# Layer 0 self-attention of a fused decoder: an earlier first unit of transposed scores, and the norm's scaling issued one step later

## The chip, the core and the metric

The kernel is one launch on one core of a Trainium2 chip. Its five engines, TensorE (PE), VectorE (DVE), ScalarE (ACT), GpSimd (POOL) and SyncE (SP, which here only starts DMAs), each run a list of instructions of their own that is fixed when the kernel is built, and wait for each other through semaphores. The metric is the device time of one execution in microseconds (us). Three runs of the kernel before have a median of 3543.11 us (3541.12 to 3548.39).

## The reference, cut to what matters

The program is a decoder of two layers over x of shape (8, 512, 256): self-attention, cross-attention and a feed-forward part in each layer, each followed by a residual add and a layer norm. The change touches only the first self-attention and its norm:

```python
def _L0_attn_ref(x, W_q, W_k, W_v, W_o, W_down_kv, W_up_k, W_up_v):
    q = x @ W_q
    k = x @ W_k
    v = x @ W_v
    latent_kv = (k + v) @ W_down_kv
    k_rec = (latent_kv @ W_up_k).reshape(b, s, H, HD).transpose(0, 2, 1, 3)
    v_rec = (latent_kv @ W_up_v).reshape(b, s, H, HD).transpose(0, 2, 1, 3)
    qh = q.reshape(b, s, H, HD).transpose(0, 2, 1, 3)
    scores = jnp.einsum('bhqd,bhkd->bhqk', qh, k_rec) / math.sqrt(d)
    decay = jnp.exp(-LAMBDA_DECAY * jnp.abs(t[:, None] - t[None, :]))
    scores = scores * decay[None, None, :, :]
    attn = jax.nn.softmax(scores, axis=-1)
    out = jnp.einsum('bhqk,bhkd->bhqd', attn, v_rec)
    return out.transpose(0, 2, 1, 3).reshape(b, s, d) @ W_o
...
x = _layernorm(x + _L0_attn_ref(x, ...), axis=-1)
```

There are 16 heads of 16 channels; the latent has 64 channels.

## The kernel before, in words

The stage works on 32 **units**: 8 batches, and in each batch 4 groups of 4 heads (`units`, in the order b, g). A unit takes four **steps**, kt = 0 to 3, one for each block of 128 keys. Everything is float32.

What one unit needs:

- `l0_prepare(b)`, once per batch and in four pieces: two turns of x (`turn`, four PE transposes of 128x128 into one PSUM tile `tT`, then an ACT copy to `xT`), `latent` (PE product with `wlat`, ACT copy) and `values` (PE product into an `s` tile, ACT copy to `vaug`). `wlat` is (W_k + W_v)^T times W_down: one DVE add of `wkT` and `wvT` (L557), eight recorded PE matmuls (L561), one DVE copy (L568).
- `l0_project` (L406 to L409): q and k of four heads by PE, two ACT copies.
- `l0_maxima(i)` (L423 to L438), for each of four blocks of 128 queries: the scores in plain layout by PE (`s_sc`, in two pairs, one `s` tile each), on each of four heads one DVE instruction that multiplies by the decay and takes the row maximum (`scored`, `mx`), then one DVE subtract that writes the block on the diagonal (`diag`, L438).
- `l0_shift` (L449 to L459): the negated maxima (DVE `mneg`), four PE transposes into `tM`, a DVE add into q (L455), and four POOL products `kr`, `kf`, `qf`, `qr` that carry the decay into q and k.
- `l0_probs(kt)` (L472 to L481): the transposed scores of one key block by PE into two `s` tiles, with the diagonal block transposed in from `diag`, and one ACT exponential for each tile (`pt`).
- `l0_values(kt)` (L492): PE adds the block's products with v to `o_pv`; the last one is copied out by ACT (`oT`, L501). `l0_finish` turns and divides.

The `s` tiles are three PSUM buffers used in turn, so each new one waits until the tile three places earlier has been read. The `tT`, `tM` and `o_out` tiles share one buffer.

**Order.** Before the loop the kernel computes `wlat`, prepares batch 0, projects units 0 and 1, takes all four maxima of unit 0, shifts it, takes all four maxima of unit 1, and projects unit 2. The loop then runs step kt of unit n as: transposed scores and exponentials of unit n; values of the step before; maxima number kt of unit n + 2; then, at kt = 1, the shift of unit n + 1; at kt = 2, `l0_finish` of unit n - 1; at kt = 0 and 3, one piece from the list `later`, and at kt = 3 also the projection of unit n + 3. `later` holds the next batch's `l0_prepare` and the last batch's `l0_output` (two turns, two products). The second product adds the residual (DVE, L541) and calls `normed(..., on_act=True)`: DVE statistics (L213, L214), a DVE add of epsilon (L215), a POOL power (`rs`, L216), a DVE product (`ve`, L218) and four ACT instructions that write the normed x (L221). Beside all this POOL runs a long chain of products for the feed-forward weights (`butterfly_ops`, L299), two or three of them per step, in a fixed order.

The four engines' lists come from a planner that sorts the instructions by priorities when the kernel is built; `tc.manual_schedule(engines={PE})` makes PE follow the order of the program inside its block, and `tc.keep_in_program_order(...)` does so for one instruction.

## Time and profile before

| what | value |
|---|---|
| median of three runs | 3543.11 us (3541.12 to 3548.39) |
| the profiled execution, time and span | 3548.88 us, of it 3547.2 us span |
| PE busy | 3332.7 us (94% of the span) |
| DVE, ACT, POOL busy | 2082.5, 1510.1, 1115.3 us (59%, 43%, 31%) |
| granted PE clock, mean | 0.965 of full |
| before the loop, up to the first transposed scores | 0 to 60.80 us |
| 28 intervals between ends of the loop's projections (82.02 to 780.15 us) | 698.13 us: PE busy 653.67, DVE 486.83, ACT 311.15, POOL 530.46 |

A row of the page or of the timeline gives the start in us, the duration, the engine, the line of the kernel, the operation, what is written and read, and how many instructions were merged; a bracket holds the idle time of the engine just ahead and what ended it. PE rows count each float32 matmul as two records. In the windows, columns are the stretch, its length, busy time and instruction count of PE, PEld (weight loads), DVE, ACT and POOL, then the granted PE clock (1.00 is full), the DMA share and GB/s. PE's ends are modelled, so a busy PE can still be a slow PE: the clock column has to be read beside it.

### The profile page before, as it was taken

The page shows a single profiled execution, that of the slowest core. Times are in us where ns is not written, and L with a number is a line of the kernel's source. Part 1 is how long each engine was busy: PE and PEld are TensorE (multiplying, and loading weights), DVE is VectorE, ACT ScalarE, POOL GpSimd, SP SyncE. Part 2 cuts the span into 40 slices and gives each one's busy share as a digit, 9 for nine tenths or more (in the row PEclk, how much of TensorE's full clock was granted, in tenths as well). Part 3 has the DMA queues.
Part 4 walks back from the last instruction along what each step waited for, and adds up shares of the span by engine and source line. Part 5 has one row for each costly group of instructions (what it writes and reads, how often), then busy time and mean ns, then how long its engine had stood idle before and what let it go on. Part 6 is the DMA issues. An engine that isn't in the chain of part 4 may idle for free. (4 is left out here: it accounts for less than half of the span.)

```text
span 3547.2 us, 52530 instructions
## 1 busy us (share of the span) xinstructions
PE 3332.7 (94%) x19574; PEld 2092.0 (59%) x19574; DVE 2082.5 (59%) x5710; ACT 1510.1 (43%) x3139; POOL 1115.3 (31%) x1032
## 2 busy tenths in 40 slices
PE   8989999998999989999999999999999998999995
PEld 3333434345666656666666666555555555888884
DVE  5777766675666556777777775666666665211012
ACT  2444444443443335655556654444444433222222
POOL 3868677772221122222222220011111111222222
PEclk8999999999999999999999999999999999999997
DMA  4100011111000079422333330000000004666674
GB/s 132 31 19 25 22 37 37 36 36 47 5 2 1 1 195 259 77 37 38 38 40 43 40 52 4 4 19 19 22 16 14 17 13 143 206 185 187 183 230 139
DMA packets 166001, 234.96 MB, mean 66 GB/s; under 512 B 26569, under 2 KB 128649, under 8 KB 165746
## 3 DMA queue, kind: packets, MB, share of 16 engines
q1 hardware_dynamic: 139010, 175.83, 15.8%
q0 software_dynamic: 25584, 51.57, 10.2%
q10 hardware_dynamic: 1152, 4.19, 0.3%
q8 instruction: 156, 2.56, 0.3%
q14 instruction: 99, 0.81, 0.1%
HBM read 135.83 MB, written 61.11 MB: 56 GB/s over the span
## 5 line engine op out<-in xcount | busy, mean ns | idle before, releaser
L428 DVE CUSTOM_DVE_ANT_0 scored<-s_sc,decay 128x512 f32<-128x512 f32 x512 | 323.5, 687 | 223.9 <-PE s_sc L423 222.7
L281 ACT ACTIVATE p<-p,nm 128x128 f32<-128x128 f32 (+3 forms) x512 | 282.5, 553 | 301.7 <-DVE nm L270 300.4
L865 POOL DMA_DIRECT2D qk<-turned x256 | 208.2, 1232 | 593.4 <-issue 304.6
L481 ACT ACTIVATE pt<-s_st 128x1024 f32<-128x1024 f32 x256 | 261.1, 1023 | 268.2 <-PE s_st L477 237.9
L902 DVE TENSOR_SCALAR p<-p,rsum 128x576 f32<-128x576 f32 (+4 forms) x768 | 300.3, 433 | 10.0
L1111 ACT ACTIVATE p<-s_sc,nm 128x576 f32<-128x576 f32 x256 | 189.6, 743 | 221.7 <-DVE nm L1110 200.8
L1477 DVE TENSOR_SCALAR y<-o_y,share 128x256 f32<-128x256 f32 x71 | 34.2, 483 | 408.9 <-PE o_y L1457 408.9
L1440 PE MATMUL s_h<-xnT,we 128*128 128x256 f32 (+1 forms) x1248 | 260.3, 362 | 0.0
L270 DVE CUSTOM_DVE_ANT_0 p<-s_sc,tabs 128x128 f32<-128x128 f32 (+3 forms) x512 | 225.1, 484 | 57.4 <-PE s_sc L925 57.3
L1457 PE MATMUL o_y<-we,h 128*128 128x256 f32 x1136 | 251.4, 379 | 0.0
L1457 PEld LDWEIGHTS o_y<-we,h 128*128 128x128 f32 x1136 | 215.3, 190 | 29.0
L1478 POOL DMA_INDIRECT total<-y,to x71 | 110.2, 1552 | 388.4 <-DVE y L1477 219.8
L1440 PEld LDWEIGHTS s_h<-xnT,we 128*128 128x128 f32 x1248 | 216.7, 191 | 24.3 <-ACT xnT L1419 0.2
L1110 DVE TENSOR_REDUCE nm<-s_sc 128x1 f32<-128x576 f32 x256 | 183.3, 748 | 72.7 <-PE s_sc L1106 71.7
L423 PE MATMUL s_sc<-k,q 32*128 32x512 f32 x1024 | 175.6, 674 | 25.8 <-ACT pt L481 23.2
L110 ACT COPY pt<-tP 128x512 f32<-128x512 f32 (+1 forms) x224 | 109.9, 491 | 208.5 <-PE tP L1123 117.7
L958 ACT COPY pt<-tP 128x384 f32<-128x384 f32 (+1 forms) x384 | 173.0, 514 | 45.3 <-PE tP L957 44.8
L925 PE MATMUL s_sc<-qk 64*128 64x128 f32 (+3 forms) x1024 | 176.8, 461 | 13.7 <-DMA qk<-turned 10.3
L1106 PE MATMUL s_sc<-k,q 64*128 64x288 f32 x1024 | 169.4, 440 | 7.7 <-ACT p L1111 7.5
L957 PE MATMUL tP<-ident,p 128*128 128x128 f32 x1280 | 169.5, 276 | 5.3 <-ACT pt L958 4.0
L957 PEld LDWEIGHTS tP<-ident,p 128*128 128x128 f32 x1280 | 144.9, 141 | 49.4 <-issue 28.0
L981 PE MATMUL o_pv<-pt,vc 128*64 128x128 f32 (+1 forms) x2304 | 167.5, 290 | 0.0
(280 smaller groups left out, 6474.0 us busy)
## 6 DMA issues: line engine op xcount, KB each, us to landing
we<-in_mo_w SPq DMA_DIRECT2D x78, 1024.0 KB, 5.5
rows_in<-zero SPq DMA_DIRECT2D x64, 530.0 KB, 13.2
qk<-turned POOLq DMA_DIRECT2D x256, 128.0 KB, 4.5
coef<-in_ff_upw SPq DMA_DIRECT2D x40, 256.0 KB, 3.3
coef<-in_ff_dnw SPq DMA_DIRECT2D x40, 256.0 KB, 3.2
xr<-rows_in SPq DMA_DIRECT2D x32, 265.0 KB, 5.7
x<-in_x SPq DMA_DIRECT2D x8, 512.0 KB, 9.9
total<-x SPq DMA_DIRECT2D x8, 512.0 KB, 2.9
```

Of the source, the lines that this page charges most:

```text
L270: dve.tensor_tensor_reduce(out=p[:, j, 0:n], in0=s[:, j, 0:n], in1=m, scale=-scale, scalar=3.0e38, op0=ALU.add, op1=ALU.min, accum_out=nm[ ...
L281: act.activation(p[:, j, 0:n], p[:, j, 0:n], AF.Exp, bias=nm[:, j : j + 1], scale=-1.0, accum_out=sums[:, at + j : at + j + 1],)
L428: dve.tensor_tensor_reduce(out=scored[:, h, :], in0=s[:, j, :], in1=decay[:, i, :], scale=1.0, scalar=-3.0e38, op0=ALU.mult, op1=ALU.max, ...
L481: act.activation(pt, s, AF.Exp, scale=1.0 / 16.0)
L865: pool.dma_start(out=qk[h : h + 32], in_=other[g : g + 32], accum_op=ALU.add)
L902: dve.tensor_scalar(p[:, j, 0:n], p[:, j, 0:n], rsum[:, j : j + 1], None, ALU.mult)
L925: pe.matmul(s[:, j, at : at + n], lhsT=q[h : h + 64, i * P : (i + 1) * P], rhs=k[h : h + 64, 0:n], start=True, stop=True,)
L957: pe.transpose(t[:, n, :], p[:, j, at * P : (at + 1) * P], ident)
L1110: dve.tensor_reduce(nm[:, j : j + 1], s, AX.XY, ALU.max, negate=True)
L1111: act.activation(p[:, j, :].rearrange("p (t n) -> p t n", t=2), s, AF.Exp, bias=nm[:, j : j + 1], accum_out=sums[:, j : j + 1])
L1440: pe.matmul(s[:, j, :], lhsT=w1[:, c, f * P : (f + 1) * P], rhs=xnT[:, c, :], start=(c == 0), stop=(c == KC - 1),)
L1457: pe.matmul(o, lhsT=h[:, f, i * P : (i + 1) * P], rhs=w2[:, f, :], start=(f == 0), stop=(f == 7),)
```

## The change

`normed` can now put its last part (the DVE product `ve` and the four ACT scalings) on a list, `scalings`, in place of running it; `l0_output` uses that, and the loop runs the part at kt = 1 of the following unit, with the ACT instructions held in program order. The exponentials are held in program order too. Ahead of the loop PE follows the program: x is turned first, then `wlat` is made; unit 1 is projected and the values of batch 0 are made between the maxima of unit 0; unit 2 is projected directly after the shift of unit 0; only two of the four maxima of unit 1 are taken ahead of the loop. The other two are taken in unit 0, which so takes 2, 2, 1 and 1 maxima in its four steps.

```diff
-    def normed(dst, r, on_act=False):
+    def normed(dst, r, on_act=False, then=None):
...
         pool.tensor_tensor(rs, ve, mhalf, ALU.pow)
-        if on_act:
-            dve.scalar_tensor_tensor(ve, mv[:, :, 0], -1.0, rs, ALU.mult, ALU.mult)
-        for i in range(NT):
+
+        def scaling(held=lambda instruction: instruction):
             if on_act:
-                act.activation(dst[:, i, :], r[:, i, :], AF.Identity, bias=ve[:, i : i + 1], scale=rs[:, i : i + 1])
-                continue
...
+                dve.scalar_tensor_tensor(ve, mv[:, :, 0], -1.0, rs, ALU.mult, ALU.mult)
+            for i in range(NT):
+                if on_act:
+                    held(
+                        act.activation(dst[:, i, :], r[:, i, :], AF.Identity, bias=ve[:, i : i + 1], scale=rs[:, i : i + 1])
+                    )
+                    continue
...
+        if then is None:
+            scaling()
+        else:
+            then.append(scaling)
...
-            act.activation(pt, s, AF.Exp, scale=1.0 / 16.0)
+            tc.keep_in_program_order(act.activation(pt, s, AF.Exp, scale=1.0 / 16.0))
...
-                normed(xs[b], r, on_act=True)
+                normed(xs[b], r, on_act=True, then=scalings)
...
-        later = []
-        for piece in l0_prepare(0):
-            piece()
-        for u in units[:2]:
-            l0_project(*u)
-        for u in units[:2]:
+        later, scalings = [], []
+        with tc.manual_schedule(engines={PE}):
+            turn0, turn1, latent, values = l0_prepare(0)
+            turn0()
+            turn1()
+            dve.tensor_tensor(wkT, wkT, wvT, ALU.add)
...
+            dve.tensor_copy(wlat.rearrange("p c n -> p (c n)"), o[:, 0 : KC * 64])
+            latent()
+            l0_project(*units[0])
+
+            between = [values, partial(l0_project, *units[1])]
             for i in range(NT):
-                l0_maxima(*u, i)
-            if u == units[0]:
-                l0_shift(*u)
-        l0_project(*units[2])
+                l0_maxima(*units[0], i)
+                if between:
+                    between.pop(0)()
+            l0_shift(*units[0])
+            l0_project(*units[2])
+
+            for i in range(2):
+                l0_maxima(*units[1], i)
         for n, (b, g) in enumerate(units):
-            ahead2 = units[n + 2] if n + 2 < len(units) else None
+
+            maxima = [(*units[n + 2], i) for i in range(NT)] if n + 2 < len(units) else []
+            if n == 0:
+                maxima = [(*units[1], i) for i in range(2, NT)] + maxima
...
-                if ahead2:
-                    l0_maxima(*ahead2, kt)
-
+                for _ in range(-(-len(maxima) // (NT - kt))):
+                    l0_maxima(*maxima.pop(0))
+
+                if kt == 1 and n + 1 < len(units):
+                    l0_shift(*units[n + 1])
                 if kt == 1:
-                    if n + 1 < len(units):
-                        l0_shift(*units[n + 1])
+
+                    if scalings:
+                        scalings.pop(0)(tc.keep_in_program_order)
...
         for piece in later:
             piece()
+        for scaling in scalings:
+            scaling()
```

As built, the two kernels hold the same instructions. Their lists differ in these places only. On PE: the part ahead of the loop and unit 0. On DVE: the `wlat` copy stands behind the three products that prepare `rise` and `fall` (L162, L164) in place of ahead of them, and the add into q of unit 0 (L455) stands directly behind `mneg`, ahead of the first four reductions of unit 1. On POOL: one add of two biases (L181) stands two places earlier, ahead of `kr` and `kf` of unit 1. On ACT: the copy of the values stands behind q and k of unit 0, and in seven places (units 8, 12, 16, 20, 24, 28 and 30, counted from 0) the four scalings stand behind the exponentials of kt = 1; before they stood ahead of the exponentials of kt = 0 in the first six and behind them in the seventh. The DVE product `ve` (L218) keeps its place. The SP list is the same.

More of the change, by code (lines that the diff above doesn't have):

```diff
@@ L216, in normed @@
         pool.tensor_tensor(rs, ve, mhalf, ALU.pow)
-        if on_act:
-            dve.scalar_tensor_tensor(ve, mv[:, :, 0], -1.0, rs, ALU.mult, ALU.mult)
-        for i in range(NT):
+        def scaling(held=lambda instruction: instruction):
             if on_act:
-                act.activation(dst[:, i, :], r[:, i, :], AF.Identity, bias=ve[:, i : i + 1], scale=rs[:, i : i + 1])
-                continue
-            dve.tensor_scalar(
-                dst[:, i, :], r[:, i, :], mv[:, i, 0:1], rs[:, i : i + 1], ALU.subtract, ALU.mult
-            )
+                dve.scalar_tensor_tensor(ve, mv[:, :, 0], -1.0, rs, ALU.mult, ALU.mult)
[5 more added lines that the diff above has]
+                    continue
+                dve.tensor_scalar(
+                    dst[:, i, :], r[:, i, :], mv[:, i, 0:1], rs[:, i : i + 1], ALU.subtract, ALU.mult
+                )
+        if then is None:
+            scaling()
+        else:
+            then.append(scaling)
     def r_tile():
@@ L556, in decoder_kernel @@
         diags = [slot(f"diag{i}").rearrange("p (i h n) -> p i h n", i=NT, h=4) for i in range(2)]
-        dve.tensor_tensor(wkT, wkT, wvT, ALU.add)
-        o = o_tile("o_wlat")
-        for c in range(KC):
-            for k in range(KC):
-                pe.matmul(
-                    o[:, c * 64 : (c + 1) * 64],
-                    lhsT=wkT[:, k, c * P : (c + 1) * P],
-                    rhs=wdown[:, k, :],
-                    start=(k == 0),
-                    stop=(k == KC - 1),
-                )
-        dve.tensor_copy(wlat.rearrange("p c n -> p (c n)"), o[:, 0 : KC * 64])
         bias_row = bfly.tile([1, 1024], F32, name="bias_row")
@@ L572, in decoder_kernel @@
         units = [(b, g) for b in range(NB) for g in range(4)]
-        later = []
-        for piece in l0_prepare(0):
-            piece()
-        for u in units[:2]:
-            l0_project(*u)
-        for u in units[:2]:
-            for i in range(NT):
-                l0_maxima(*u, i)
-            if u == units[0]:
-                l0_shift(*u)
-        l0_project(*units[2])
+        later, scalings = [], []
[4 more added lines that the diff above has]
+            dve.tensor_tensor(wkT, wkT, wvT, ALU.add)
+            o = o_tile("o_wlat")
+            for c in range(KC):
+                for k in range(KC):
+                    pe.matmul(
+                        o[:, c * 64 : (c + 1) * 64],
+                        lhsT=wkT[:, k, c * P : (c + 1) * P],
+                        rhs=wdown[:, k, :],
+                        start=(k == 0),
+                        stop=(k == KC - 1),
+                    )
+            dve.tensor_copy(wlat.rearrange("p c n -> p (c n)"), o[:, 0 : KC * 64])
+            latent()
+            l0_project(*units[0])
+            between = [values, partial(l0_project, *units[1])]
+            for i in range(NT):
+                l0_maxima(*units[0], i)
[5 more added lines that the diff above has]
+                l0_maxima(*units[1], i)
         for n, (b, g) in enumerate(units):
-            ahead2 = units[n + 2] if n + 2 < len(units) else None
+            maxima = [(*units[n + 2], i) for i in range(NT)] if n + 2 < len(units) else []
+            if n == 0:
+                maxima = [(*units[1], i) for i in range(2, NT)] + maxima
             if g == 0 and b + 1 < NB:
```

## The prediction

> **What bounds the kernel now.** I read the engine totals first: PE is busy 94% of the span, so time is to be found where PE stands still or runs slowly. The chain of waits lists only pieces from 2343 us on, so for this stage I cut the loop at the end of each unit's projection (the ACT row of L409) and asked for busy time and granted clock in each interval. Three neighbours, the middle one holding a norm:

> ```profile
> 223.74:246.50 22.76, 22.39 (x154) 9.86 (x154) 17.11 (x45) 10.34 (x14) 19.03 (x15) 1.00 0.10 27
> 246.50:276.51 30.01, 25.86 (x161) 11.03 (x159) 18.62 (x46) 12.26 (x17) 19.55 (x16) 0.89 0.10 27
> 276.51:299.09 22.58, 22.33 (x151) 9.11 (x151) 16.79 (x42) 10.91 (x15) 19.23 (x15) 1.00 0.04 13
> ```

> A unit is PE's work and nothing else (22.33 of 22.58 us). With the norm it takes 30.01, and the clock falls to 0.89. The other five intervals like it take 31.22, 30.69, 30.71, 30.73 and 29.96: six sum to 183.32. The waits of the loop and the timeline of that interval say why:

> ```profile
> ACT x L221 <- DVE ve L218: 30.0, 6, 5.0
> PE s_sc L423 <- ACT pt L481: 23.2, 6, 3.9
> ```

> ```profile
> 250.22 0.30 PEld L423 LDWEIGHTS s_sc<-k,q 32*128 32x128 f32 x4 [0.84 <-issue]
> ...
> 250.94 1.23 DVE L218 SCALAR_TENSOR_TENSOR ve<-mv,rs 128x4 f32<-128x4 f32 x1 [1.15 <-POOL rs L216]
> 252.21 2.08 ACT L221 ACTIVATE x<-r,ve,rs 128x256 f32<-128x256 f32 x4 [5.02 <-DVE ve L218]
> 254.19 1.91 ACT L481 ACTIVATE pt<-s_st 128x1024 f32<-128x1024 f32 x2
> 255.25 2.08 PE L423 MATMUL s_sc<-k,q 32*128 32x512 f32 x4 [3.90 <-ACT pt L481]
> ```

> ACT reaches the scaling at 247.2, waits 5.02 us for `ve`, scales for 2.08, and only then takes the exponentials of kt = 0, whose input was ready near 249.2. They free the `s` tile that the second pair of plain scores needs, so PE stands 3.90 us. Then a second price: the granted clock, by the microsecond, falls from 1.00 to 0.50 inside 253 to 254 and is back inside 260 to 261. The waiting costs 3.9, the slow clock most of the rest.

> The second place is the start. DVE's first reduction begins at 30.30, and the loop's first transposed scores at 60.80; between them DVE is nearly full and PE's clock half:

> ```profile
> 30.30 0.69 DVE L428 CUSTOM_DVE_ANT_0 scored<-s_sc,decay 128x512 f32<-128x512 f32 x1 [16.39 <-PE s_sc L423]
> ...
> 43.69 0.17 DVE L449 TENSOR_REDUCE mneg<-mx 128x16 f32<-128x16 f32 x1
> ...
> 60.80 0.93 PE L475 MATMUL s_st<-qf,kr 32*128 32x384 f32 x8
> ```

> **1. The scaling behind kt = 1 (units 8, 12, 16, 20, 24, 28).** As built, only the four ACT scalings move; `ve` keeps its DVE place, so its 1.15 us of waiting for POOL and its 1.23 us stay, with four reductions behind it. ACT's exponentials of kt = 0 start at about 249.2. The scaling falls into the idle time between the exponentials of kt = 1 and kt = 2, which in this very unit is 2.73 us (the exponential at 270.63 waits that long for PE), against 2.08 us needed: hidden, 0.65 to spare. `ve` is some 5 us old by then. Without that cover it would cost up to 2.08 per unit. No DMA and no POOL instruction moves with it.

> What is late next is DVE: the norm's add, statistics and `ve` fill 247.89 to 252.1, and PE could give it scores at about 251.4. So the first pair's tile comes free 0.7 us late for the transposed scores of kt = 1. In addition `diag` (L438) then falls among POOL's products of 250.87 to 257.08, a dense run; such meetings show as rows of 2.6 to 3.3 us in place of 0.7, and a unit with one took 23.85 where 22.6 is usual. So a unit with a norm costs between 22.5 (unit 4, same turns of x and no norm: 22.49) and 25 (two such meetings at 23.85 - 22.6 = 1.25 each); I take 22.6 + 0.7 for the late DVE + 0.3 for a chance of a meeting = **23.6**. Six: 183.32 - 141.6 = **-41.7**; ends -48 and -33.

> **2. Unit 30.** There the stall is PE's 2.73 us behind the same scaling (808.27), with no fall of the clock. Behind kt = 1 the scaling meets an ACT that idles only 0.5 to 0.8 us between exponentials, since no maxima are left. Of 2.08 us some 1.3 shows: 2.73 - 1.3 = **-1.4**; ends 0 and -2.7.

> **3. The start, x first.** The landing of x is not in the trace; its DMA was issued ahead of `wvT`, which landed at 7.42, so PE can turn x some 2 us sooner. That is worth nothing: the `wlat` copy on DVE (0.29 us, at 10.17 before) now stands behind the three products for `rise` and `fall`, whose last waits for its DMA and ends at 13.91. `latent` starts at about 14.25 in place of 13.45: **+0.8**.

> From there PE has `latent` (3.67 at the slow rate), q (3.67) and k (1.12): k ends near 22.7, ACT's copies near 23.9 (as 26.23 to 27.44 before), scores at 24.0, first reduction at **25.15** in place of 30.30; unit 1's projection (3 us) and the values (3.9 us) are out of the way. Unit 0's maxima take DVE 13.4 us (30.30 to 43.69), if PE keeps up with values and unit 1's projection between them: 5.0 us of PE at full clock, 8.5 at half, against about 2.2 us per maximum to spare, so 0.5 to 4.5 us of DVE idle. `mneg` then at 39.2 to 43; I take **40**.

> The add into q now directly follows `mneg` on DVE: it waits for `tM` (1.3 us), with unit 1's reductions queued behind it. Unit 2's projection on PE (3.1 us, or 4.8 at half clock) comes ahead of unit 1's scores, so DVE is idle some 4 us there that before were covered. Then two maxima, 6.8 us on DVE; the transposed scores need the tile freed after the third pair, about 10 us after `mneg`: kt = 0 near **51** in place of 60.8. But two maxima come back inside: kt = 0 and kt = 1 take 6.8 us of DVE each where PE needs 6.1 (5.0 a step plus 1.14 of plain scores), behind what DVE still owes. From 51, DVE ends them near 66, and the tile for kt = 2 is free 2 us sooner. kt = 2 starts near 64 in place of 68.89. **-4.5** for the start, the +0.8 inside it; ends 0 and -9.

> The POOL add that moved waits for its DMA to 33.1 as before; `kr` and `kf` of unit 1 behind it are not read until unit 1's first step, 30 us later: nothing. The values' ACT copy moves behind q and k, where ACT idles: nothing. Pinning the exponentials leaves their order as it was.

> [...] **Row first:** PE was busy from 13.45 with gaps below 0.7 us, yet matmuls of 128x512 ran at about 0.91 us each until 25 us, and at half that after it; and the clock fell at 35 while PE showed 96% busy, with no wait above 2.5 us:

> ```profile
> 30.00:35.00 5.00, 3.65 (x16) 0.90 (x12) 4.52 (x14) 0.41 (x1) 3.52 (x4) 1.00 0.90 255
> 35.00:40.00 5.00, 4.82 (x14) 1.74 (x16) 4.79 (x16) 0.00 (x0) 0.00 (x0) 0.52 0.47 170
> ```

> [...]

> **4. The other DVE and POOL meetings.** [...]

> ```profile
> 193.43 9.27 DVE L438 TENSOR_TENSOR diag<-scored,mx 128x512 f32<-128x512 f32 x1
> ```

> This one got through only when POOL stopped at 202.15, after seven products in a row. Its interval, like one other (9.37 us at 422.22), took 29.21 in place of 22.6: +6.6. Faster units leave POOL less slack (19 of 22.6 us instead of 19.5 of 30). [...] POOL's list is the same and meets q's wait in every unit, so I count none new and none gone.

> **Sum:** -41.7 - 1.4 - 4.5 = **-47.6**. Against the profiled execution (3548.88) this gives 3501; that lies 5.8 above the median shown, 3543.11, from which it gives 3495.5. I predict **3496**, with 3484 to 3510 for this case alone (the ends above, partly together).

> **Rivals.**

> - *DVE takes ACT's place.* `ve` still stands ahead of the reductions; if the late reductions and POOL's run cost PE 3 us per unit and the clock falls briefly, units take 26 to 27: 183.3 - 159 = -24, with the start -28: **3515**. For it: 4.2 us of norm work at kt = 0. [...] 0.13.
> - *More than I count.* The two long meetings vanish with the shifted start (-13): **3482**. Against: they lie nine units apart, which is 90 POOL products at ten per unit, or five whole stages of 18: a pattern that repeats. 0.08.
> - *The loop gets slower.* Place: `diag` at L438; price 6.6; it decides from eight new long meetings on. At one in each second unit, 15 new: +99 - 47.6, **3594**. For it: POOL's shorter slack. Against: 22 plain units already run at this density with two such rows. 0.04.
> - *The scalings are not what stalls* (another wait stands behind them): only the start is left, **3539**. Against: the chain ACT to PE above, and the same 5.0 us six times. 0.02.

> The likeliest gets 0.73. The range **3481 to 3516** takes in the first two rivals' times. What a measurement of this kernel can tell is about 0.2%, or 7 us: faster 0.94, the same 0.02, slower 0.04.

> **What would show it.** Right: the intervals of units 8, 12, ... at 23 to 25 us with a clock of 1.00; no wait of PE's plain scores for `pt` near 3.9 us; the scaling right behind the exponentials of kt = 1; the first reduction near 25, the first transposed scores near 51. Wrong: these intervals above 26 us, a clock below 1.00 in them, PE waiting for `mx` at kt = 1, more `diag` rows above 9 us, or a first reduction that is not earlier than 28.

## The result, and the profile after

The changed kernel takes 3506.44 us (median of four runs, 3503.39 to 3513.75) against 3545.32 us (3541.12 to 3548.39) for the kernel before, measured beside it: a ratio of 0.9904, 95% interval 0.9883 to 0.9925. The forecast was 3496, range 3481 to 3516. The profiled execution took 3503.39 us, span 3501.7 against 3547.2, granted PE clock 0.973 against 0.965. Most line numbers of the stage moved by 9: the plain scores are now L432, `mx` L437, `diag` L447, the transposed scores L481 and L484; `ve` moved by 2 to L220, the scaling by 3 to L224.

First the windows of the changed kernel, cut at the loop's projections as before (at the start of the ACT copy of k): the same norm unit, its plain neighbour, the interval with the second long `diag` row, and the last of the six norm units.

```profile
243.28:267.46 24.18, 22.86 (x161) 9.89 (x159) 19.61 (x46) 12.39 (x17) 20.04 (x16) 1.00 0.11 34
267.46:290.04 22.58, 22.33 (x151) 9.12 (x151) 16.81 (x42) 10.92 (x14) 19.23 (x15) 1.00 0.05 13
407.26:437.28 30.02, 25.84 (x154) 11.06 (x154) 25.00 (x46) 10.32 (x13) 18.13 (x15) 0.89 0.06 16
715.29:741.12 25.83, 23.97 (x157) 9.69 (x155) 19.06 (x47) 11.80 (x17) 20.20 (x16) 0.93 0.10 31
```

The norm unit went from 30.01 us at clock 0.89 to 24.18 at 1.00. The six are 24.18, 24.16, 24.15, 24.16, 24.16 and 25.83: together 146.64 in place of 183.32, **-36.7**. The last one still loses clock. The third row is a plain unit that got no faster at all: behind a `diag` of 9.39 us PE waited 3.91 us for `mx`, and the granted clock was at half from 416.67 to 423.50, so that part of what such a row costs is slow clock.

The timeline inside the norm unit, to be laid beside the rows of before:

```profile
247.72 1.25 DVE L220 SCALAR_TENSOR_TENSOR ve<-mv,rs 128x4 f32<-128x4 f32 x1 [1.15 <-POOL rs L216]
...
250.25 0.38 PE L481 MATMUL s_st<-qr,kf 32*128 32x128 f32 x2 [1.08 <-DVE mx L437]
...
253.77 2.06 ACT L224 ACTIVATE x<-r,ve,rs 128x256 f32<-128x256 f32 x4
...
256.61 1.03 ACT L490 ACTIVATE pt<-s_st 128x1024 f32<-128x1024 f32 x1 [0.78 <-PE s_st L486]
```

The scaling now starts with no wait, takes its 2.06 us behind the exponentials of kt = 1, and the next exponential still has to wait 0.78 us for PE: it is fully hidden. PE's wait of 3.90 us for `pt` is gone. What is late next is DVE: `ve` keeps its 1.15 us of waiting, the four reductions behind it come late, and PE waits 1.08 us for `mx`.

The start of the changed kernel:

```profile
14.08 3.50 PE L386 MATMUL o_lat<-xT,w 128*64 128x512 f32 x4 [4.63 <-DVE w L586]
17.51 1.98 PE L415 MATMUL s_qk<-xT,w 128*128 128x512 f32 x4
...
22.99 0.69 DVE L437 CUSTOM_DVE_ANT_0 scored<-s_sc,decay 128x512 f32<-128x512 f32 x1 [9.06 <-PE s_sc L432]
...
39.90 3.62 PE L415 MATMUL s_qk<-xT,w 128*128 128x512 f32 x4
...
48.92 0.92 PE L484 MATMUL s_st<-qf,kr 32*128 32x384 f32 x4 [0.19 <-DVE mx L437]
...
53.24 5.56 PE L432 MATMUL s_sc<-k,q 32*128 32x512 f32 x16
...
66.02 0.69 DVE L437 CUSTOM_DVE_ANT_0 scored<-s_sc,decay 128x512 f32<-128x512 f32 x1 [3.89 <-PE s_sc L432]
...
69.03 0.70 PE L481 MATMUL s_st<-qr,kf 32*128 32x256 f32 x4
```

Reductions begin 7.3 us sooner and transposed scores 11.9 us sooner, yet unit 0 ends at 84.61, where it ended at 82.02 before. The rows say where it goes: q's projection of unit 0 took 1.98 us at 17.51, the same four matmul records for unit 2 took 3.62 us at 39.90, the plain scores of two maxima in kt = 0 (at 53.24) took 5.56 us, and in the middle of unit 0 DVE, which has two maxima per step to do, waits 3.89 us for plain scores. The last row is the start of kt = 2. The windows of this stretch show the clock beside it (third figure from the right end):

```profile
30.97:34.38 3.41, 2.50 (x12) 0.60 (x8) 3.09 (x9) 0.39 (x1) 1.43 (x2) 1.00 0.81 243
...
34.00:39.00 5.00, 0.01 (x1) 0.01 (x1) 4.76 (x11) 0.00 (x0) 2.56 (x2) 0.54 0.69 217
...
48.03:51.44 3.41, 2.05 (x11) 0.63 (x8) 3.23 (x10) 0.00 (x0) 0.00 (x0) 1.00 0.02 5
...
55.00:60.00 5.00, 5.00 (x20) 1.89 (x16) 4.45 (x12) 0.11 (x1) 0.00 (x0) 0.50 0.00 0
60.00:65.00 5.00, 5.00 (x32) 2.35 (x36) 2.10 (x8) 1.71 (x3) 0.00 (x0) 0.50 0.00 0
```

The clock halves twice: at 34.38, at the beginning of an idle gap of PE (33.7 to 39), and at 51.44, after which it stays at half (0.50 from 51.44 to 65.08) through most of unit 0's first two steps, while PE shows as fully busy. In the 3.41 us ahead of each fall (the first and third row) PE was busy for 2.50 and 2.05 us, with products of 32 rows.

By intervals, after against before in the two profiled executions:

| place | us |
|---|---|
| start, to the end of unit 0 | +2.59 |
| six norm units | -36.68 |
| interval of unit 6 (first long `diag` row: 9.27 us before, 5.71 after) | -5.86 |
| interval of unit 15 (second long row: 9.37 before, 9.39 after) | +0.81 |
| the other units of the loop | +0.11 |
| units 29 to 31, to the last `oT` copy | -2.95 |
| behind the stage | -3.5 |
| span | -45.5 |

### The profile page after: what moved, and what is told of

Read it like the earlier page. It is cut to its first block, busy times and chain, and to the rows that moved or that the text cites. A ratio compares the mean times of both kernels' runs of the same rounds, so it can differ in the third digit from the quotient of the medians.

```text
span 3501.7 us, 52528 instructions
## 1 busy us (share of the span) xinstructions
PE 3299.3 (94%) x19574; PEld 2080.0 (59%) x19574; DVE 2087.4 (60%) x5710; ACT 1510.5 (43%) x3139; POOL 1118.1 (32%) x1032
## 5 line engine op out<-in xcount | busy, mean ns | idle before, releaser
L437 DVE CUSTOM_DVE_ANT_0 scored<-s_sc,decay 128x512 f32<-128x512 f32 x512 | 323.0, 687 | 179.6 <-PE s_sc L432 178.8
L1481 PE MATMUL o_y<-we,h 128*128 128x256 f32 x1136 | 251.4, 379 | 0.0
L1134 DVE TENSOR_REDUCE nm<-s_sc 128x1 f32<-128x576 f32 x256 | 183.3, 749 | 73.0 <-PE s_sc L1130 72.1
L447 DVE TENSOR_TENSOR diag<-scored,mx 128x512 f32<-128x512 f32 x128 | 167.5, 1309 | 2.4
```

Source lines behind the costliest of these rows:

```text
L437: dve.tensor_tensor_reduce(out=scored[:, h, :], in0=s[:, j, :], in1=decay[:, i, :], scale=1.0, scalar=-3.0e38, op0=ALU.mult, op1=ALU.max, ...
L1134: dve.tensor_reduce(nm[:, j : j + 1], s, AX.XY, ALU.max, negate=True)
L1481: pe.matmul(o, lhsT=h[:, f, i * P : (i + 1) * P], rhs=w2[:, f, :], start=(f == 0), stop=(f == 7),)
```

## The experiments

Each ratio is against the kernel before, measured beside it. "Unit 0 ends" is the start of the ACT copy of k of the projection made in unit 0 (82.02 before, 84.61 after).

**The scaling alone.** The start is that of before (`wlat` ahead of x, all eight maxima ahead of the loop); the scaling stays behind kt = 1.

```diff
-        with tc.manual_schedule(engines={PE}):
-            turn0, turn1, latent, values = l0_prepare(0)
...
+        for piece in l0_prepare(0):
+            piece()
+        for u in units[:2]:
+            l0_project(*u)
+        for u in units[:2]:
             for i in range(NT):
-                l0_maxima(*units[0], i)
...
+                l0_maxima(*u, i)
+            if u == units[0]:
+                l0_shift(*u)
+        l0_project(*units[2])
...
-            if n == 0:
-                maxima = [(*units[1], i) for i in range(2, NT)] + maxima
```

> The scaling behind kt = 1, with the old start. If the six norm units carry the gain (183.32 us before, 146.64 after, in the two profiles) and the new start costs 2.6 us (unit 0 ends at 84.61 in place of 82.02): 37 to 42 us faster than before, and 0 to 4 us faster than the changed kernel; norm units at 24.1 to 24.2 us with a clock of 1.00. If the new start gains the 4.5 us of the prediction after all, further on: 4 to 5 us slower than the changed kernel.

Measured: 3510.55 against 3549.63, ratio 0.9893 (0.9866 to 0.9919). That is 39.1 us by the medians, as expected. The norm units take 24.14 to 24.19 and 25.77. The whole gain that can be measured is in the scaling.

**The start alone.** The new start; the scaling runs where it did.

```diff
-                normed(xs[b], r, on_act=True, then=scalings)
+                normed(xs[b], r, on_act=True)
```

> The new start alone, with the old place of the scaling. If the start gives back what it gains inside unit 0: first reduction near 23, first transposed scores near 49, but unit 0's last copy of k at 84 to 85 (82.02 before), and the whole time within 3 us of before, on the slow side. If the prediction's start holds: 4.5 us faster than before. The six norm units stay at 30 to 31 us in both.

Measured: 3554.8 against 3549.63, ratio 1.0011 (1.0001 to 1.002): nothing gained. By the medians it is 5.2 us slower, where at most 3 were expected. Unit 0 ends at 84.12. The norm units are back at 29.75 to 31.39 (the first of them at a clock of 0.89), so pinning the exponentials does nothing by itself.

**The `wlat` copy first.** The changed kernel with the products for `rise` and `fall` behind the `wlat` copy on DVE.

```diff
-    dve.tensor_scalar(rise, rise, float(np.exp(0.01 * (S - 1))), None, ALU.mult)
-    for t in (fall, rise):
-        dve.tensor_scalar(t, t, noaug, aug, ALU.mult, ALU.add)
...
             dve.tensor_copy(wlat.rearrange("p c n -> p (c n)"), o[:, 0 : KC * 64])
+            for t in (fall, rise):
+                if t is rise:
+                    tc.keep_in_program_order(dve.tensor_scalar(t, t, float(np.exp(0.01 * (S - 1))), None, ALU.mult))
+                tc.keep_in_program_order(dve.tensor_scalar(t, t, noaug, aug, ALU.mult, ALU.add))
```

> The changed kernel with the wlat copy ahead of the products for rise and fall on DVE. If that place on DVE is what takes the profit of turning x first: latent starts near 9.9 in place of 14.08, the first reduction near 19 in place of 22.99. [...]

Measured: `latent` at 9.97 in place of 14.08, first reduction at 19.47 in place of 22.99, unit 0 ends at 79.29, 5.3 sooner. So it is this copy that eats what turning x first could bring. More came back than the 4 us of the chain, because the falls of the clock came at other times too (the windows of 5 us from 30 to 70 us show 0.66, 0.66, 1.00, 0.52, 0.50, 0.61, 1.00 and 0.66), so this run does not part the chain from the clock. In the whole time, 0.9889 (0.9867 to 0.991), it can't be told from the changed kernel.

**PE kept busy.** The changed kernel with ten more products of 128x128 by 512 columns that nobody reads, in PE's idle time: two behind the third maximum of unit 0, four behind the fourth, two behind each of unit 1's.

```diff
+            warm = o_tile("o_warm")
+
+            def idle_products(n):
+                for _ in range(n):
+                    pe.matmul(warm, lhsT=ident, rhs=wq0[:, 0, 0:512], start=True, stop=True)
...
                 if between:
                     between.pop(0)()
+                else:
+                    idle_products(2 if i == 2 else 4)
...
                 l0_maxima(*units[1], i)
+                idle_products(2)
```

> The changed kernel with ten added products of 128x128 by 512 columns on PE, which nobody reads, between the plain scores ahead of the loop. If the slow clock ate the start's gain: the clock stays at 1.00 from 34 to about 58 us, DVE's waits for plain scores in unit 0 (2.5, 3.9 and 2.8 us) fall below 4 us in sum, and unit 0 ends 3 to 6 us earlier than 84.61, though PE has 10 us more to do. If DVE's two added maxima in unit 0 are the bound: the clock rises, but unit 0 ends within 1.5 us of 84.61 or later.

The windows of this kernel, over two of the stretches of the changed one:

```profile
34.00:39.00 5.00, 3.67 (x12) 1.64 (x11) 4.00 (x12) 0.00 (x0) 1.74 (x2) 1.00 0.40 149
...
55.00:60.00 5.00, 4.54 (x36) 1.71 (x36) 3.34 (x11) 2.05 (x2) 0.00 (x0) 1.00 0.00 0
```

The clock stays at 1.00 to near 65 us (0.96 from 60 to 65), PE passes 36 records from 55 to 60 us where it passed 20, and the three DVE waits for plain scores in unit 0 sum to 5.1 us in place of 9.2 (below 4 was expected). Unit 0 ends at 77.53, 7.1 us sooner, with more work on PE. One microsecond of that lies ahead of the first reduction (21.99 in place of 22.99), where a DMA that `rise` waits for landed sooner; from the first reduction to the end of unit 0 it is 55.5 us in place of 61.6. So half clock costs this start some 6 us. That its order has a share too is shown by the first of the versions below. Whole time 0.9874 (0.9851 to 0.9896); this interval overlaps that of the changed kernel, so at this size only the trace shows the gain, and only in unit 0: unit 28 ends at 741.26, as in the changed kernel (741.12), because a long `diag` row cost it 29.91 us in the interval of unit 6 in place of 23.35.

**The norm's product later.** The kernel with the scaling alone, and `ve` pinned on DVE behind the maxima of kt = 0.

```diff
+        def last_product(held=lambda instruction: instruction):
+            held(dve.scalar_tensor_tensor(ve, mv[:, :, 0], -1.0, rs, ALU.mult, ALU.mult))
...
-            then.append(scaling)
+            then.extend([last_product, scaling])
...
+                if kt == 0 and scalings:
+                    scalings.pop(0)(tc.keep_in_program_order)
```

> As the scaling alone (old start), with the norm's last DVE product behind the maxima of kt = 0 in place of ahead of them. If the 1.6 us that a norm unit still takes over a plain one (24.16 against 22.58) are DVE's late reductions, PE's wait of 1.08 us for the first pair at kt = 1 shrinks below 0.3 and the norm units fall to 23.0 to 23.3 us; unit 28, which also falls into the slow clock (25.8), to about 23: some 6 to 9 us in all. If what is left is the norm's own PE work and the meeting of diag with POOL, they stay at 24 or above.

The same norm unit in its windows:

```profile
240.90:264.39 23.49, 22.86 (x161) 9.89 (x159) 19.07 (x46) 12.49 (x18) 20.04 (x16) 1.00 0.14 35
```

All six take 23.49, the last one too, at a clock of 1.00. PE's busy time in this unit is 22.86 as in the changed kernel; its longest wait for `mx` is 0.4 in place of 1.08 (below 0.3, and units of 23.0 to 23.3, were expected). Whole time 0.9886 (0.9869 to 0.9902).

**POOL nearly free.** The kernel with the scaling alone; the products for the feed-forward weights run behind the loop, so only the loop is comparable (the whole took 3873.75).

```diff
-                for _ in range(3 - kt % 2):
-                    next(butterfly, None)
```

> As the scaling alone (old start), with all of POOL's butterfly products taken out of the loop and run after it. Only the loop can be compared. If the diag rows of 2 to 9 us are DVE waiting for POOL: every diag row below 0.8 us, the two intervals of 23 to 30 us (units 6 and 15) at 22.6 to 23.3, unit 11 at 22.7, norm units about 0.5 us shorter. If they come from something else, rows above 2 us stay at the same units.

The tile's own view of `diag` gives count, then shortest, middle and longest duration in ns; below it this kernel's window of unit 6, whose interval held the first long row.

```profile
L447 DVE TENSOR_TENSOR diag<-scored,mx x128: 683/692/1696, 28.3 to 744.1; 128x512 f32<-128x512 f32 x128
```

```profile
193.67:216.96 23.29, 22.67 (x160) 9.72 (x158) 14.87 (x40) 11.45 (x14) 5.39 (x4) 1.00 0.00 1
```

With POOL busy 5.39 us in this unit in place of 19 to 20, no `diag` takes more than 1.70 us (below 0.8 was expected). The two intervals of 29.21 of before take 23.29 and 22.63, and every norm unit takes 23.49 or 23.50, unit 28 too, although `ve` stands early: its wait for POOL is what made it late.

**Versions meant to be better.** The first has x and the `wlat` copy first, all eight maxima ahead of the loop with the shift of unit 0 behind unit 1's first, unit 2 projected last, and `ve` behind kt = 0. The second adds two unread products behind each of the last six maxima. The third adds to that one tiny POOL product per unit that waits for the last `diag`, to make POOL pause. The first edit shown is the start of the second version against the changed kernel, without the lines on `wlat` and `ve`; the other is what the third adds.

```diff
-            l0_shift(*units[0])
-            l0_project(*units[2])
-
-            for i in range(2):
+                else:
+                    idle_products(2)
+            for i in range(NT):
                 l0_maxima(*units[1], i)
+                idle_products(2)
+                if i == 0:
+                    l0_shift(*units[0])
+            l0_project(*units[2])
```

```diff
+                if kt == 3 and n + 2 < len(units):
+                    d = live["diag", units[n + 2][0], units[n + 2][1]][0:1, 3, 0, 0:4]
+                    tc.keep_in_program_order(pool.tensor_tensor(behind, d, d, ALU.mult))
```

> A version from the findings: x turned first, wlat copied ahead of rise and fall, all eight maxima ahead of the loop as in the kernel before, unit 2 projected last, the norm's product behind the maxima of kt = 0 and its scaling behind kt = 1. First reduction near 19.5, first transposed scores at 48 to 51, unit 0 ends at 71 to 76 (84.61 in the changed kernel, 82 to 83.4 with the old start). With the norm units at 23.1: 12 to 18 us faster than the changed kernel. If the start is bound by PE's slow clock and not by DVE's 27 us of reductions, unit 0 ends at 78 or later.

> The same with two products of 128x128 by 512 columns, which nobody reads, behind each of the last six maxima ahead of the loop. If the slow clock costs in that version: the clock stays at 1.00 through the start and unit 0 ends 1 to 4 us earlier than without them. If DVE hides it: within 1 us, or later.

> As the last version (early start, busy PE, product behind kt = 0), with one small POOL product per unit that reads the diag block of kt = 3, so that POOL pauses there until DVE has written it. If the two long diag rows (9.3 us at units 5 and 14) come from POOL's unbroken run of products, they fall to 5 us or below, the intervals of units 6 and 15 from 29.8 to 23 to 25, and the kernel gains 8 to 13 us. If POOL's pause costs as much as it saves, or the rows move to other units, no gain.

| kernel | unit 0 ends | norm units | long rows | unit 28 ends | median, before | ratio (95%) |
|---|---|---|---|---|---|---|
| eight maxima early | 72.28 | 23.48 to 23.50 | 9.28, 9.37 | 729.34 | 3500.66, 3546.41 | 0.9878 (0.986 to 0.9896) |
| and PE kept busy | 70.50 | 23.48 to 23.50 | 9.28, 9.37 | 727.63 | 3493.98, 3546.41 | 0.9852 (0.9833 to 0.9871) |
| and POOL pauses | 70.99 | 23.49 to 23.50 | none above 3.4 | 726.44 | 3497.75, 3548.96 | 0.9854 (0.9833 to 0.9875) |

One stretch of the first and then of the second shows what the unread products do:

```profile
35.00:40.00 5.00, 4.59 (x16) 1.95 (x16) 4.86 (x15) 0.00 (x0) 4.00 (x4) 0.50 0.49 179
```

```profile
35.00:40.00 5.00, 5.00 (x22) 1.88 (x21) 4.96 (x15) 0.00 (x0) 2.05 (x2) 1.00 0.35 127
```

Yet at full clock unit 0 ends only 1.8 us sooner: here DVE is nearly full either way (4.86 and 4.96 of 5.00), and the clock was worth little here. The first of these versions and the kernel with the `wlat` copy first differ in their start by the order alone, and in both the clock was at half for over 20 us of it (in this one 0.51 from 30 to 35, 0.50 from 35 to 50 and 0.94 from 50 to 55); from the first reduction to the end of unit 0 they took 53.4 and 59.8 us. With the unread products it was 50.8 and 55.5. So the order with all eight maxima ahead of the loop and unit 2 projected last is worth 6.4 us against the new one at half clock, and some 5 with the clock kept up. The pauses of POOL removed both long rows (-6.6 and -4.3 us in their intervals) and gave most of it back in four other units, which took 1.3 to 2.9 us more each; net -1.7 in the loop, and nothing in the whole time. The first version was expected to be 12 to 18 us faster than the changed kernel; by the ratios it is about 9, and the intervals overlap. The second version is the best found, and its interval lies below that of the changed kernel. All kernels with `ve` later lose something in units 29 to 31, which took them 48.6 to 50.9 us from the end of unit 28 to the last `oT` copy, against 47.3 in the changed kernel and 50.2 before; why stays open.

**The changed kernel again**, without an edit, measured beside the last version.

> The changed kernel once more, for a comparison with that version on the same chip: 0.988 to 0.992 of the time before. In the profile the start, the norm units and unit 28 as in its first profile (84 to 85, 24.2 and 25.8 us); the long diag rows of units 5 and 14 may be there or not.

Measured: 3515.27 against 3548.96, ratio 0.9904 (0.9884 to 0.9923), as the first time. Its profile is not as the first time. Unit 0 ends at 87.39, not 84.61, where 84 to 85 was expected, and unit 28 at 753.37, not 741.12. The changed kernel's first profiled execution has this timeline of `diag` and of the POOL products that it meets:

```profile
196.06 5.71 DVE L447 TENSOR_TENSOR diag<-scored,mx 128x512 f32<-128x512 f32 x1
196.20 2.46 POOL L308 TENSOR_TENSOR wup<-wup,coef 128x512 f32<-128x512 f32 x2
...
201.08 1.81 POOL L308 TENSOR_TENSOR wup<-wup,coef 128x512 f32<-128x512 f32 x1
```

and the repeat this:

```profile
200.41 9.28 DVE L447 TENSOR_TENSOR diag<-scored,mx 128x512 f32<-128x512 f32 x1
200.56 2.46 POOL L308 TENSOR_TENSOR wup<-wup,coef 128x512 f32<-128x512 f32 x2
...
205.44 1.25 POOL L308 TENSOR_TENSOR wup<-wup,coef 128x512 f32<-128x512 f32 x1
...
207.88 1.25 POOL L468 TENSOR_TENSOR kf<-k,w 128x512 f32<-128x512 f32 x1
```

The same instructions: POOL works without a break, and `diag` begins 0.14 and 0.15 us ahead of the product shown in the second row. (The dots in each stand for two more products of `wup`, in the second also for `kr`.) Once `diag` is through during the fifth product, which then takes 1.81 in place of 1.25, once it is through only behind the seventh. Interval 23.35 the first time, 29.75 in the repeat.

## Why the prediction was right, and where not

- **The scaling** (-41.7 forecast, -36.7 measured): the mechanism was right at each step. It sits where it was put, is hidden with 0.78 us to spare (0.65 forecast), PE's wait for `pt` is gone, and with it the fall of the clock in five of six units. The term mis-sized is the norm unit's 23.6: it takes 24.16. With `ve` later, or POOL free, it takes 23.49: 0.67 of it is `ve` waiting for POOL, close to the 0.7 I gave DVE's lateness as a whole. The other 0.9 above a plain unit stays in both those kernels; 0.53 of it is PE work (22.86 busy against 22.33), which the base of 22.6 had left out. And the six are not alike: in unit 28 PE waits 1.41 us for `mx` in place of 1.08, and there the clock does fall for a moment (0.93 in its window): 25.83. With `ve` later it does not. So the rival that puts DVE in ACT's place comes near in one unit of six. Two of the signs of being wrong that I had listed did show: PE waits for `mx` at kt = 1 in all six units, and in unit 28 the clock is below 1.00; both cost less than the rival put on them.
- **Unit 30** (-1.4): units 29 to 31 gained 2.95, beyond the end I gave, -2.7. The two traces show which size was off: I let 1.3 us of the scaling show. From the first transposed scores of kt = 2 to those of kt = 3 PE took 3.03 us in place of 6.46, and after that only the eight records of kt = 3 were longer, 1.39 us in place of 0.93.
- **The start** (-4.5 forecast, +2.6 at the end of unit 0). Every step up to the first transposed scores held or was beaten: `latent` at 14.08 (14.25 forecast), first reduction at 22.99 (25.15, mostly since q took 1.98 us where 3.67 was reckoned), `mneg` at 38.76 (40), first transposed scores at 48.92, their second tile at 51.01 (51). The step that failed is "kt = 2 starts near 64": it started at 69.03. I had priced the clock into the part ahead of the loop and then reckoned unit 0's steps at full clock, with two maxima each as DVE's work alone. At half clock the sixteen records of plain scores in kt = 0 took 5.56 us, DVE waited 2.47 us for them and 3.89 for the next, and the 11.9 us of lead at the first transposed scores were gone by kt = 2 (68.89 before). The kernel with PE kept busy shows what the clock costs here, some 6 us. The order has a share of its own: with all eight maxima ahead of the loop and unit 2 projected last, the way from the first reduction to the end of unit 0 took 6.4 us less, at half clock for over 20 us all the same. Which of the moved pieces is worth how much was not taken apart. That unit 0 ends later than with the old start is no chance of one execution: 84.12, 84.61 and 87.39 in three of the new start, 82.02 to 83.41 in four of the old.
- **The clock at the start.** q's projection of unit 0 took 1.98 us in the changed kernel and 3.67 in the kernel before (at 21.50), with a granted clock of 1.00 in both (16 to 34 us, and 10 to 35), and 3.15 in the repeat; what sets its time is not shown. For the later part I took the half clock of before (0.52 from 35 to 40), and that held: 0.50 from 34.38 to 44.62. But I had read the row wrong: the 96% are PE's share in the five microseconds behind the fall; in the five ahead of it PE was busy 3.65 of 5.00, 73%. In the 3.41 us ahead of the falls it was busy for 2.50 and 2.05 us in the changed kernel and 2.26 (31.77 to 35.18) in the one before; what makes the clock fall is not shown by that. The -4.5 did not come out: it left out what half clock costs inside unit 0.
- **The long meetings** ("none new and none gone"): in the profiled execution the first one shrank from 9.27 to 5.71, which is -5.9 us of its interval, and the repeat had it back at 9.28. In the other kernels above whose loop has the full POOL list it was 5.72, 5.72, 2.06, 0.84 or 9.28, while the second was 9.35 to 9.39 in all but the one with the start alone (0.91). In every one of these traces the first `diag` begins 0.13 to 0.16 us ahead of the next POOL product, whatever the start was: POOL and DVE meet at the same point, and 0.84, 2.06, 5.7 and 9.28 us come out of it in no order of that distance. So nothing here shows that the shift of the start decides these meetings; the rival in which both vanish came up in one execution, of the kernel with the start alone, and not in either of the changed kernel. In the repeat the `diag` of 9.28 us lay beside seven POOL instructions in a row. That POOL's products are the cause is shown by their removal (no row above 1.70 us).
- **The sum.** -47.6 forecast; -42.0 at the end of the stage: 7.1 lost at the start, 5.0 in the norm units, 1.6 found in units 29 to 31, and 5.05 in the two long meetings (0.1 elsewhere). By the medians the whole gained 38.9, and the forecast of 3496 lies below all four runs. That the sum at the end of the stage came within 5.6 us is in part luck: the misses at the start and in the norm units, 12.1 us together, were more than half offset by units 29 to 31 and by a long row that was short in this execution and back in the next.

**Open:** the part behind the stage, whose code is the same, took 2712.6 to 2723.7 us from the last `oT` copy in the kernels above other than the one with POOL nearly free (before: 2716.8). In the kernel with the start alone unit 28 ends 8.1 us sooner than before, and the whole takes no less. Gains of 5 to 7 us at the start are therefore seen in the trace and not in the times, and I can't say whether part of them is lost again later. Why one `diag` gets through between two POOL products and the other does not is not settled either.

## What to carry to other kernels

Here a scaling that waited 5.02 us for its input on ACT held back exponentials whose input was ready near 249.2 until 254.19. Ask what stands behind an instruction that waits for a slow chain, and place it where its input is old and its engine idles anyway, here worth 6 us each six times for four scalings moved by one step. Reckon a stretch at the clock that the trace grants in it, and carry that clock on into what follows: a lead of 11.9 us was gone here behind two steps that ran at half clock. And before calling a difference of one interval an effect, look whether the same code shows it twice.
